# Layer 0's mixing by banks: each bank's first tiles followed by mixes of other tiles, two of four row statistics on the scalar engine, accumulators in the transposes' PSUM banks

## The chip, the cores and the metric

The kernel runs on one core of a Trainium2 chip. The metric is the time on the device in microseconds (us) of one execution; of several executions the median is taken. A core has five engines with instruction queues of their own, each worked off in order: PE (matrix products; PEld is its weight load), DVE (vector), ACT (scalar functions and copies), POOL (general, here elementwise work), and SP, which here only issues DMA transfers. They meet through semaphores. [...]

## The reference, cut to what matters

Two layers, each with a mixing (attention) and a feed-forward part, all with residuals, on x of 4 x 512 x 1024. The change is in the first part of layer 0 alone:

```
x = x + mix(layernorm(x))                 # the change is here
def mix(h):                               # h: 4 x 512 x 1024
    q = transpose(h, (2, 0, 1))           # 1024 columns, each 4 x 512
    prob = softmax(einsum('lnc,lmc->lnm', q, q) / sqrt(512))   # 4 x 4 for each column
    return h + transpose(einsum('lnm,lmc->lnc', prob, q), (1, 2, 0))
x = x + ffn0(layernorm(x))                # starts with normalise, transpose, matmul
```

For each of the 1024 columns the four batch rows are scored against one another over the 512 positions, and mixed by the softmax of the 4 x 4 scores.

## The kernel before, in words

x stays in SBUF as 16 tiles of 128 rows x 1024 columns: batch n (4) by position tile j (4), tile index 4n + j. For each j the four batches' rows are normalised into h (`normed_tiles`), with columns of the four batches side by side, in 32 groups of 128 (32 columns x 4 batches).

*Grams and turned h.* For each j, PE adds h·h of each group into `grams` (`gram`, L328), four PSUM banks g0 to g3 of 8 groups, and transposes each group (`turn`, L319) by four per PSUM bank (`pt`, 4 banks); ACT copies each bank into hTA (groups 0 to 19) or hTB (20 to 31) (L322). At the last j all grams are summed first, and then the eight turns follow.

*Weights.* `weights(gram)` makes the softmax of a bank on DVE: masked and reduced scores (L218, L222), maximum and difference (L224, L226), Exp on ACT (L227), sum, reciprocal, product with the reciprocal (pr, L233), plus the identity (L234), spread over halves (L236). `turned(halves, k)` expands half a bank into wt (L244), 128 x 512, for k = 0 on DVE and for k = 1 on POOL, lets PE transpose it (L252) and ACT copy it to w (L254). There are eight such w, q = 0 to 7; each has four groups.

*Mixing.* `mix(q, w, j)` is four products of hT with w into a PSUM tile of one bank (`ps`, L263) and an addition of it into x on DVE (L266). There are 8 x 4 = 32 of them. `ps` has 4 buffers that turned weights and mixes take in rotation: a buffer is free again once ACT has copied it or DVE has added it. The order: for each bank the weights, then for its two q the turn and the mix of tile j = 0 of the q before (L363 to L373); then the tiles j = 1 to 3 of q = 0 to 4 (the ones that read hTA), with the row statistics for the next layernorm of tiles n, j = 0 between them on DVE (`statistic`, L134: two bn_stats of 512 columns and their aggregate); then nine mixes of q = 5 to 7, which read hTB (L392).

*What lies beside it.* The feed-forward weights w0 come in 8 chunks of 128 x 1160 (`load_split`, L176): DMA to a staging tile, a cast to w_h on ACT (L182), the remainder w_l on POOL (L185). Chunks 0 to 3 use two staging buffers, so a transfer waits for POOL to have split the chunk two before. Chunks 4 to 7 and the first two normalised tiles (L141, L391) lie in the memory of hTA, so they wait for the last mix that reads hTA; they have three staging buffers. All four POOL wt come ahead of the splits in POOL's queue. The first feed-forward matmuls (L150 to L152, `matmul3`) need the transposes of a normalised tile (L163), a cast of these on ACT (L145) and the remainder hTl on DVE (L146); they take chunks 0 to 3 for all columns and then chunks 4 to 7.

*What sets the order.* The program is written through a scheduler that places instructions in each engine's queue by its own estimate; `tc.issue_after(i)` holds an instruction's place behind i in that order, and is no wait on the chip. `tops`, `wts`, `exps`, `rooted` are lists of instructions that such places refer to.

Of the kernel before, what the change touches and what calls it, by code (L numbers as in the profile page):

```python
# [17 lines left out]
P = 128  # L18
# [28 lines left out]
def block_kernel(ctx: ExitStack, tc: tile.TileContext, a: dict, out: bass.AP):  # L47
# [47 lines left out]
    def rsqrt(v, n, eps, name="y2", bufs=3):  # L95
# [10 lines left out]
        return y2  # L106

    def statistics(xs, tag="", bufs=3, junk=(), behind=None, gates=()):


        n = len(xs)
        mv = small.tile([P, n, 2], F32, name=f"mv{tag}", bufs=bufs)
        for k, xt in enumerate(xs):
            if k < len(junk):
                nm = small.tile([P, 1], F32, name="nm")
                with tc.issue_after(gates[0].ins) if gates else ExitStack():
                    A.activation(junk[k], xt, AF.Identity, scale=-1.0 / D, accum_out=nm)
                sq = small.tile([P, 1], F32, name="sq")
                A.activation(junk[k], xt, AF.Square, bias=nm, accum_out=sq)
                V.tensor_scalar(mv[:, k, 0:1], nm, -1.0, None, ALU.mult)  # L120
                V.tensor_scalar(mv[:, k, 1:2], sq, 1.0 / D, None, ALU.mult)
                continue
            st = small.tile([P, 2, 6], F32, name="st")
            for c in range(2):
                with tc.issue_after(gates[1].ins) if gates else ExitStack():
                    V.bn_stats(st[:, c, :], xt[:, c * 512 : (c + 1) * 512])
            summed = V.bn_aggr(mv[:, k, :], st)
        with ExitStack() if tag else tc.high_priority():
            if behind is not None:
                with tc.issue_after(summed.ins):  # L130
                    behind()
            return mv, rsqrt(mv[:, :, 1], n, 1e-5, f"rstd{tag}", bufs)
# [67 lines left out]
    with tc.tile_pool(name="a_hTB", bufs=1) as hTBp, tc.tile_pool(name="a_WB", bufs=GB // 4) as WBp, \  # L200
# [6 lines left out]
        def hT(g):  # L207
            return hTA[:, g, :] if g < GA else hTB[:, g - GA, :]

        exps = []  # L210
        tops, wts = [], []

        def weights(gram):
# [12 lines left out]
            tops.append(V.tensor_tensor(ex, sc, top.to_broadcast([P, GBK, NB]), ALU.subtract))  # L226
            exps.append(A.activation(ex, ex, AF.Exp, scale=1.0 / math.sqrt(S)))  # L227
            den = small.tile([P, GBK, 1], F32, name="den")
# [11 lines left out]

        def turned(halves, k, psp, Wp, eng):

            wt = wk.tile([P, 8 * NB, GL], F32, name="wt", bufs=3)
            made = eng.tensor_tensor(  # L244
                wt, halves[:, 4 * k : 4 * k + 4].rearrange("p g b m -> p (g b m)").unsqueeze(2)
                .to_broadcast([P, 8 * NB, GL]),
                same_col.unsqueeze(1).to_broadcast([P, 8 * NB, GL]), ALU.mult)
            wts.append(made)
            wt = wt.rearrange("p (g k) l -> p g (k l)", g=4)
            ps = psp.tile([P, 4, P], F32, name="ps")  # L250
            for g in range(4):
                T.transpose(ps[:, g, :], wt[:, g, :], ident)  # L252
            w = Wp.tile([P, 4, P], F32, name="w")
            A.copy(w, ps)  # L254
            return w, made

        xv = x.rearrange("p (n j) (k l) -> p j k n l", n=NB, l=GL)

        def mix(q, w, j, psp):

            ps = psp.tile([P, 4, P], F32, name="ps")
            for g in range(4):
                T.matmul(ps[:, g, :], lhsT=hT(4 * q + g)[:, j * P : (j + 1) * P], rhs=w[:, g, :],  # L263
                         start=True, stop=True)
            xs = xv[:, j, 8 * q : 8 * q + 8]
# [4 lines left out]
        with tc.tile_pool(name="a_h", bufs=2) as hp, tc.tile_pool(name="a_junk", bufs=1) as junkp:  # L270
# [3 lines left out]
            with tc.tile_pool(name="a_pt", bufs=4, space=PSUM, side="right") as ptp:  # L274
# [39 lines left out]
                for j in range(TPB):  # L314
# [17 lines left out]
                    if j == TPB - 1:  # L332


                        for q in range(NQ):
                            gram(q)
                        for q in range(NQ):
                            turn(q)
                        break
# [20 lines left out]

        with tc.tile_pool(name="a_ps", bufs=4, space=PSUM) as psp:
            ws = []
            for k, gram in enumerate(grams):  # L363
                halves = weights(gram)
                for i in range(2):
                    q = 2 * k + i
                    w, last_wt = turned(halves, i, psp, WAp if q < NQA else WBp, (V, G)[i])
                    ws.append(w)


                    if q > 0:
                        mix(q - 1, ws[q - 1], 0, psp)
            mix(NQ - 1, ws[NQ - 1], 0, psp)  # L373
            with tc.issue_after(exps[-1].ins):
                A.activation(first, first, AF.Sqrt)
            with tc.issue_after(last_wt.ins):
                load_w0(w0p, range(ND // 2), 2, (G, G))
            mv = small.tile([P, NB, 2], F32, name="mv", bufs=3)
            for k, (q, j) in enumerate((q, j) for q in range(NQA) for j in range(1, TPB)):
                mix(q, ws[q], j, psp)  # L380
                if k % 2 and k // 2 < NB:
                    statistic(mv, x[:, k // 2 * TPB, :], k // 2)
            stats0 = {0: (mv, rsqrt(mv[:, :, 1], NB, 1e-5, "rstd", 3))}
# [8 lines left out]
            for j in range(1, TPB):  # L392
                for q in range(NQA, NQ):
                    mix(q, ws[q], j, psp)
        psA.close()
        psB.close()
# [1333 lines left out]
```

## Time and profile before

| what | value |
|---|---|
| median of 3 runs | 1747.36 us (1746.56 to 1749.04) |
| the profiled execution, its own time | 1748.09 us |
| its span, first to last instruction | 1746.3 us |
| mean granted clock of PE over the span | 0.999 |
| end of layer 0's last transposes (L319) | 45.27 us |
| first turn of the weights (L252) | 46.32 us |
| first feed-forward transposes (L163) | 82.64 us |
| first feed-forward matmul (L150) | 85.19 us |

Times in the trace count from the first instruction. A line of a timeline is: start, length, engine, line of the program, operation, what it writes and reads, the shapes, how many were merged; in brackets, how long the engine was idle before it and what ended that. A PE record is one pass; an f32 product of 128 x 128 by 128 has two. A DVE length contains about 0.09 us that the next, independent operation overlaps: adds into x of 0.69 follow each other every 0.60. An operation of DVE or POOL that stands still after it was started is drawn as long, not as a gap. In the windows, the columns are: stretch, its length, busy time of PE, PEld, DVE, ACT, POOL with counts, PE's clock, the share of DMA and GB/s.

### The profile page before, as it was taken

The page shows a single profiled execution, that of the slowest core. Times are in us where ns is not written, and L with a number is a line of the kernel's source. Part 1 is how long each engine was busy: PE and PEld are TensorE (multiplying, and loading weights), DVE is VectorE, ACT ScalarE, POOL GpSimd, SP SyncE. Part 2 cuts the span into 40 slices and gives each one's busy share as a digit, 9 for nine tenths or more (in the row PEclk, how much of TensorE's full clock was granted, in tenths as well). Part 3 has the DMA queues.
Part 4 walks back from the last instruction along what each step waited for, and adds up shares of the span by engine and source line. Part 5 has one row for each costly group of instructions (what it writes and reads, how often), then busy time and mean ns, then how long its engine had stood idle before and what let it go on. Part 6 is the DMA issues. An engine that isn't in the chain of part 4 may idle for free.

```text
span 1746.3 us, 31628 instructions
## 1 busy us (share of the span) xinstructions
PE 1707.5 (98%) x10536; PEld 1429.7 (82%) x10536; DVE 1302.4 (75%) x3494; ACT 905.0 (52%) x2316; POOL 921.9 (53%) x926
## 2 busy tenths in 40 slices
PE   7999999999999999999999999999999999999999
PEld 6899999998677777767777767777767777789998
DVE  7977885676777777787777687777778776687675
ACT  7422331366765555575555575555476555453332
POOL 0553541203665665566566556566556655675454
PEclk9999999999999999999999999999999999999999
DMA  4313543245334234353333353342454333853431
GB/s 194 135 42 115 185 159 114 89 138 169 106 99 140 81 118 140 113 172 117 110 112 119 110 193 95 106 139 94 131 169 151 102 110 109 309 201 123 137 105 74
DMA packets 131939, 228.16 MB, mean 131 GB/s; under 512 B 22272, under 2 KB 58752, under 8 KB 128448
## 3 DMA queue, kind: packets, MB, share of 16 engines
q1 hardware_dynamic: 131776, 226.13, 39.2%
q8 instruction: 84, 1.38, 0.3%
q14 instruction: 79, 0.65, 0.1%
HBM read 156.60 MB, written 71.83 MB: 131 GB/s over the span
## 4 chain that ended last, share of the span: by engine, by line
PE 88%; DVE 5%; POOL 4%; ACT 2%; issue 1%; DMA 0%; POOLq 0%; ACTq 0%; DVEq 0%
PE psv L958 8%; PE pst L942 7%; PE po L150 4%; PE po L152 4%; PE po L151 4%; PE pss L150 4%; PE pss L151 3%; PE pss L152 3%; PE pob L150 3%; PE poa L150 3%; PE psq L150 3%; PE psq L152 3%; PE psq L151 3%; PE acc L150 3%; PE acc L152 3%; PE acc L151 3%
## 5 line engine op out<-in xcount | busy, mean ns | idle before, releaser
L921 ACT ACTIVATE p<-p,mn 128x512 f32<-128x512 f32 (+3 forms) x512 | 284.9, 559 | 211.4 <-DVE mn L918 210.8
L732 POOL TENSOR_TENSOR qf<-qf,ropeT 64x512 f32<-64x512 f32 x128 | 164.4, 1285 | 259.1 <-ACT qf L728 249.3
L918 DVE CUSTOM_DVE_ANT_0 p<-pss,causal 128x512 f32<-128x512 f32 (+3 forms) x512 | 232.7, 485 | 19.8 <-PE pss L152 15.8
L942 PE MATMUL pst<-ident,p 128*128 128x128 f32 x1280 | 185.9, 273 | 1.8 <-ACT pT L944 1.7
L733 POOL TENSOR_TENSOR qf<-qf,t 64x512 f32<-64x512 f32 x128 | 164.3, 1284 | 32.0 <-DVE t L731 23.8
L942 PEld LDWEIGHTS pst<-ident,p 128*128 128x128 f32 x1280 | 153.0, 141 | 29.6 <-ACT pT L944 4.8
L944 ACT COPY pT<-pst 128x512 f32<-128x512 f32 x256 | 142.1, 579 | 31.4 <-PE pst L942 29.5
L741 POOL TENSOR_TENSOR ql<-qf,qh 128x384 fp32r<-128x384 f32 x128 | 129.6, 1013 | 53.0 <-DVE qh L740 53.0
L150 PE MATMUL pss<-kT,ql 128*128 128x512 f32 (+2 forms) x384 | 143.6, 374 | 4.4 <-POOL ql L741 4.2
L993 POOL TENSOR_TENSOR cxl<-s,cxh 128x256 fp32r<-128x256 f32 x128 | 98.1, 773 | 85.2 <-ACT cxh L992 53.9
L150 PE MATMUL po<-w_h,hTl 128*128 128x384 f32 (+1 forms) x384 | 133.1, 347 | 0.7 <-DVE x L433 0.6
L151 PE MATMUL pss<-kT,qh 128*128 128x512 f32 (+2 forms) x384 | 130.4, 340 | 0.0
L152 PE MATMUL po<-w_h,hTh 128*128 128x384 f32 (+1 forms) x384 | 130.1, 339 | 0.0
L152 PE MATMUL pss<-kT,qh 128*128 128x512 f32 (+2 forms) x384 | 129.9, 338 | 0.0
L151 PE MATMUL po<-w_l,hTh 128*128 128x384 f32 (+1 forms) x384 | 129.7, 338 | 0.0
L944 DVE COPY pT<-pst 128x256 f32<-128x256 f32 x128 | 54.1, 423 | 97.8 <-PE pst L942 97.2
L728 ACT COPY qf<-psq 128x512 f32<-128x512 f32 x126 | 73.9, 587 | 69.7 <-PE psq L152 68.0
L730 DVE TENSOR_TENSOR t<-psq,ropeT 32x512 f32<-32x512 f32 x126 | 87.7, 696 | 24.5 <-ACT qf L728 20.2
L921 ACT ACTIVATION_READ_ACCUMULATOR p<-p,mn 128x1 f32 x512 | 97.2, 190 | 0.0
L150 PEld LDWEIGHTS pss<-kT,ql 128*128 128x128 f32 x384 | 72.1, 188 | 29.1 <-POOL ql L741 9.2
L731 DVE TENSOR_TENSOR t<-psq,ropeT 32x512 f32<-32x512 f32 x126 | 87.1, 691 | 1.7
L1035 DVE TENSOR_TENSOR xs<-xs,pob 128x512 f32<-128x512 f32 x105 | 71.1, 677 | 19.0 <-PE pob L152 18.8
(567 smaller groups left out, 4975.0 us busy)
## 6 DMA issues: line engine op xcount, KB each, us to landing
xs<-x_d SPq DMA_DIRECT2D x128, 256.0 KB
x_d<-xs SPq DMA_DIRECT2D x128, 256.0 KB
slotC<-in_woT_dram SPq DMA_DIRECT2D x32, 512.0 KB
rb<-r_d SPq DMA_DIRECT2D x128, 128.0 KB
w_t<-raw SPq DMA_DIRECT2D x32, 288.0 KB
x<-in_x_dram SPq DMA_DIRECT2D x16, 512.0 KB
x_d<-x SPq DMA_DIRECT2D x32, 256.0 KB
slotA<-q_d SPq DMA_DIRECT2D x8, 1024.0 KB
```

The costliest lines, as they stand in the source:

```text
L150: T.matmul(ps, lhsT=al, rhs=bh, start=start, stop=False, **kw)
L151: T.matmul(ps, lhsT=ah, rhs=bl, start=False, stop=False, **kw)
L152: T.matmul(ps, lhsT=ah, rhs=bh, start=False, stop=stop, **kw)
L732: G.tensor_tensor(f[mid], f[mid], ropeT[mid, 0, :], ALU.mult)
L733: G.tensor_tensor(f[mid], f[mid], t2[mid], ALU.add)
L741: G.tensor_tensor(l, f[:, P:S], f32(h), ALU.subtract)
L918: turn_of[0] = V.tensor_tensor_reduce(out=to, in0=ps[:, 0:n], in1=causal[:, S - n : S], scale=1.0, scalar=-NEG, op0=ALU.add, op1=ALU.min, ...
L921: A.activation(to, to, AF.Exp, bias=mn[:, i : i + 1], scale=-1.0, accum_out=rs[:, i : i + 1])
L942: T.transpose(ps[:, w : w + P], p[:, OF[i] + j * P : OF[i] + (j + 1) * P], ident)
L944: copy(pT[:, AT[js[0]] : AT[js[0]] + w], ps[:, 0:w])
L958: T.matmul(ps[n * KVR : (n + 1) * KVR, S - w : S], lhsT=k[:, j, :], rhs=pTs[u + n][:, AT[j] : AT[j] + w], start=(j == 0), stop=(j == TPB - 1))
L993: G.tensor_tensor(l, src, f32(h), ALU.subtract)
```

## The change

- `turned` is split: `expand` makes wt, `turned` transposes and copies it. The weights of the first two banks and the expansions of the first are written ahead of the last j's turns, so ACT's Exp of the second bank comes amid the copies of these.
- The loop over the banks: both turns of a bank, the two mixes of tile j = 0, then (except for the last bank) the next bank's weights and expansions and four mixes of other tiles of q = 0 to 3. The expansions of the last bank are both on DVE; POOL makes three wt instead of four.
- The first four chunks of w0 are loaded in two halves, at the first and the third bank. In POOL's queue the order becomes: two wt, the splits of chunks 0 and 1, the third wt, the splits of chunks 2 to 7. In ACT's queue the casts of chunks 0 and 1 come behind the first bank's two w copies and the third bank's Exp; the casts of chunks 2 and 3 come behind the second bank's w copies, the fourth bank's Exp and the table load, and ahead of the third bank's w copies.
- The statistics of n = 1 and 3 go to ACT (`act_statistic`: a pass for the mean, a pass for the squares, both into a PSUM tile that is not read), those of n = 0 and 2 stay on DVE. Three mixes of q = 4 stand between them. On DVE the two normalises for the feed-forward part come behind the additions of five of the nine last mixes, with four additions behind them (before: ahead of all nine).
- `ps` is allocated from the right side of PSUM, so that its four buffers take the transposes' banks in the transposes' order (before: from the left, in the opposite order).
- The number of products, of additions and of transfers is the same. Behind the first feed-forward matmul the order of every engine's instructions is the one before.

```diff
@@ -208,7 +211,7 @@
             return hTA[:, g, :] if g < GA else hTB[:, g - GA, :]
 
         exps = []
-        tops, wts = [], []
+        tops, wts, mixed, copied = [], [], [], []
 
         def weights(gram):
 
@@ -224,7 +227,8 @@
             V.tensor_reduce(top, sc, AX.X, ALU.max)
             ex = wk.tile([P, GBK, NB], F32, name="ex")
             tops.append(V.tensor_tensor(ex, sc, top.to_broadcast([P, GBK, NB]), ALU.subtract))
-            exps.append(A.activation(ex, ex, AF.Exp, scale=1.0 / math.sqrt(S)))
+            with tc.issue_after(copied[2 * len(exps) - 3].ins) if copied else ExitStack():
+                exps.append(A.activation(ex, ex, AF.Exp, scale=1.0 / math.sqrt(S)))
             den = small.tile([P, GBK, 1], F32, name="den")
             V.tensor_reduce(den, ex, AX.X, ALU.add)
             rden = small.tile([P, GBK, 1], F32, name="rden")
@@ -238,21 +242,24 @@
                             ALU.mult)
             return halves
 
-        def turned(halves, k, psp, Wp, eng):
+        def expand(halves, k, eng):
 
             wt = wk.tile([P, 8 * NB, GL], F32, name="wt", bufs=3)
-            made = eng.tensor_tensor(
+            wts.append(eng.tensor_tensor(
                 wt, halves[:, 4 * k : 4 * k + 4].rearrange("p g b m -> p (g b m)").unsqueeze(2)
                 .to_broadcast([P, 8 * NB, GL]),
-                same_col.unsqueeze(1).to_broadcast([P, 8 * NB, GL]), ALU.mult)
-            wts.append(made)
-            wt = wt.rearrange("p (g k) l -> p g (k l)", g=4)
+                same_col.unsqueeze(1).to_broadcast([P, 8 * NB, GL]), ALU.mult))
+            return wt.rearrange("p (g k) l -> p g (k l)", g=4)
+
+        def turned(wt, psp, Wp):
+
             ps = psp.tile([P, 4, P], F32, name="ps")
             for g in range(4):
-                T.transpose(ps[:, g, :], wt[:, g, :], ident)
+                with tc.issue_after(mixed[0].ins) if mixed else ExitStack():
+                    T.transpose(ps[:, g, :], wt[:, g, :], ident)
             w = Wp.tile([P, 4, P], F32, name="w")
-            A.copy(w, ps)
-            return w, made
+            copied.append(A.copy(w, ps))
+            return w
 
         xv = x.rearrange("p (n j) (k l) -> p j k n l", n=NB, l=GL)
 
@@ -260,8 +267,9 @@
 
             ps = psp.tile([P, 4, P], F32, name="ps")
             for g in range(4):
-                T.matmul(ps[:, g, :], lhsT=hT(4 * q + g)[:, j * P : (j + 1) * P], rhs=w[:, g, :],
-                         start=True, stop=True)
+                last = T.matmul(ps[:, g, :], lhsT=hT(4 * q + g)[:, j * P : (j + 1) * P],
+                                rhs=w[:, g, :], start=True, stop=True)
+            mixed[:] = [last]
             xs = xv[:, j, 8 * q : 8 * q + 8]
             V.tensor_tensor(xs, xs, ps.rearrange("p g c -> p (g c)")
                             .rearrange("p (k n l) -> p k n l", n=NB, l=GL), ALU.add)
@@ -334,8 +342,11 @@
 
                         for q in range(NQ):
                             gram(q)
+                        halves = weights(grams[0])
+                        pairs = [[expand(halves, i, (V, G)[i]) for i in range(2)]]
+                        halves = weights(grams[1])
                         for q in range(NQ):
-                            turn(q)
+                            turn(q, exps[1] if q >= NQ // 2 else None)
                         break
                     for q in range(NQ // 2):
                         turn(q)
@@ -358,28 +369,40 @@
                     w0.append(load_split(pool, stage, a["w0"][ch], [P, W0_COLS[-1][1]], f"w0{ch}",
                                          engines[ch % 2]))
 
-        with tc.tile_pool(name="a_ps", bufs=4, space=PSUM) as psp:
+
+        with tc.tile_pool(name="a_ps", bufs=4, space=PSUM, side="right") as psp:
             ws = []
-            for k, gram in enumerate(grams):
-                halves = weights(gram)
+            others = [(q, j) for q in range(4) for j in range(1, TPB)]
+            for k in range(len(grams)):
                 for i in range(2):
-                    q = 2 * k + i
-                    w, last_wt = turned(halves, i, psp, WAp if q < NQA else WBp, (V, G)[i])
-                    ws.append(w)
-
-
-                    if q > 0:
-                        mix(q - 1, ws[q - 1], 0, psp)
-            mix(NQ - 1, ws[NQ - 1], 0, psp)
+                    ws.append(turned(pairs[k][i], psp, WAp if 2 * k + i < NQA else WBp))
+                for q in (2 * k, 2 * k + 1):
+                    mix(q, ws[q], 0, psp)
+                if k + 1 == len(grams):
+                    break
+
+                if k > 0:
+                    halves = weights(grams[k + 1])
+                pairs.append([expand(halves, i, (V, G)[i and k < 2]) for i in range(2)])
+                if k in (0, 2):
+                    with tc.issue_after(wts[2 * k + 1].ins):
+                        load_w0(w0p, range(k, k + 2), 2, (G, G))
+                for q, j in others[4 * k : 4 * k + 4]:
+                    mix(q, ws[q], j, psp)
+            psA.close()
             with tc.issue_after(exps[-1].ins):
                 A.activation(first, first, AF.Sqrt)
-            with tc.issue_after(last_wt.ins):
-                load_w0(w0p, range(ND // 2), 2, (G, G))
+
             mv = small.tile([P, NB, 2], F32, name="mv", bufs=3)
-            for k, (q, j) in enumerate((q, j) for q in range(NQA) for j in range(1, TPB)):
-                mix(q, ws[q], j, psp)
-                if k % 2 and k // 2 < NB:
-                    statistic(mv, x[:, k // 2 * TPB, :], k // 2)
+            room = psB.enter_context(tc.tile_pool(name="a_jk", bufs=1, space=PSUM))
+            aj = room.tile([P, D], F32, name="aj")
+            for n in range(NB):
+                if n % 2:
+                    act_statistic(mv, x[:, n * TPB, :], n, aj)
+                else:
+                    statistic(mv, x[:, n * TPB, :], n)
+                if n:
+                    mix(4, ws[4], n, psp)
             stats0 = {0: (mv, rsqrt(mv[:, :, 1], NB, 1e-5, "rstd", 3))}
             aside.close()
             hp = wpools.enter_context(tc.tile_pool(name="b_h", bufs=2, side="right"))
@@ -392,7 +415,6 @@
             for j in range(1, TPB):
                 for q in range(NQA, NQ):
                     mix(q, ws[q], j, psp)
-        psA.close()
         psB.close()
 
 
```

More of the change, by code (lines that the diff above doesn't have):

```diff
@@ L106, in rsqrt, with act_statistic @@
         return y2
+    def act_statistic(mv, xt, k, junk, gates=()):
+        nm = small.tile([P, 1], F32, name="nm")
+        with tc.issue_after(gates[0].ins) if gates else ExitStack():
+            A.activation(junk, xt, AF.Identity, scale=-1.0 / D, accum_out=nm)
+        sq = small.tile([P, 1], F32, name="sq")
+        A.activation(junk, xt, AF.Square, bias=nm, accum_out=sq)
+        V.tensor_scalar(mv[:, k, 0:1], nm, -1.0, None, ALU.mult)
+        V.tensor_scalar(mv[:, k, 1:2], sq, 1.0 / D, None, ALU.mult)
     def statistics(xs, tag="", bufs=3, junk=(), behind=None, gates=()):
@@ L114, in statistics @@
             if k < len(junk):
[L115 to L121, printed above, removed]
+                act_statistic(mv, xt, k, junk[k], gates[:1])
                 continue
```

## Prediction

> **What bounds the kernel now.** I read the page's shares first. TensorE (PE) is busy 98% of the span and 88% of the chain that ended last is its own work, so a microsecond counts only if PE stands still for it or runs at a lower clock.
>
> ```profile
> PE 1707.5 (98%) x10536; PEld 1429.7 (82%) x10536; DVE 1302.4 (75%) x3494; ACT 905.0 (52%) x2316; POOL 921.9 (53%) x926
> ...
> PE 88%; DVE 5%; POOL 4%; ACT 2%; issue 1%; DMA 0%; POOLq 0%; ACTq 0%; DVEq 0%
> ```
>
> The change lies between the end of layer 0's transposes (45.27 us in the trace) and the first feed-forward matmul (85.19); behind that each engine's order of instructions is the old one. Next I read the windows there (PE, PEld, DVE, ACT, POOL busy, then PE's clock) and PE's timeline.
>
> ```profile
> 49.00:57.00 8.00, 6.42 (x43) 6.42 (x44) 7.04 (x15) 4.82 (x8) 4.40 (x4) 0.79 0.10 42
> 57.00:74.00 17.00, 17.00 (x154) 17.00 (x154) 16.16 (x32) 4.28 (x6) 10.19 (x4) 1.00 0.23 72
> ```
>
> ```profile
> 46.32 1.09 PE L252 MATMUL ps<-ident,wt 128*128 128x128 f32 x8 [1.05 <-ACT hTB L322]
> 47.71 1.16 PE L263 MATMUL ps<-w,hTA 128*128 128x128 f32 x8 [0.29 <-ACT w L254]
> 50.58 1.04 PE L252 MATMUL ps<-ident,wt 128*128 128x128 f32 x4 [1.71 <-DVE wt L244]
> ...
> 61.20 13.56 PE L263 MATMUL ps<-w,hTA 128*128 128x128 f32 x120
> 74.60 8.20 PE L263 MATMUL ps<-w,hTB 128*128 128x128 f32 x72
> 82.64 1.04 PE L163 MATMUL pt<-ident,h 128*128 128x128 f32 x8
> 84.78 0.66 PE L163 MATMUL pt<-ident,h 128*128 128x128 f32 x4 [1.10 <-DVE hTl L146]
> ```
>
> From 57 on PE has no gap, and one mix (8 records) takes 0.893 us (120 records in 13.4). A turn (4 records) takes 0.437. Eight turns and 32 mixes are 3.5 + 28.6 = 32.1 us; the stretch 45.27 to 82.64 has 37.4. So 5.3 us can be won at most: 3.05 of gaps, and the clock of 0.79 behind the 1.71 us gap, 8 x 0.21 = 1.7 us.
>
> Last I read VectorE (DVE) against GpSimd (POOL). First POOL's timeline, then DVE's:
>
> ```profile
> 56.63 5.28 POOL L185 TENSOR_TENSOR w_l<-stage,w_h 128x1160 fp32r<-128x1160 f32 x2
> ...
> 80.10 10.59 POOL L185 TENSOR_TENSOR w_l<-stage,w_h 128x1160 fp32r<-128x1160 f32 x4 [8.77 <-ACT w_h L182]
> 90.64 1.27 POOL L484 TENSOR_TENSOR raw<-raw 128x288 fp32r<-128x288 f32 x1
> ```
>
> ```profile
> 75.65 1.54 DVE L141 TENSOR_SCALAR h<-x,mv,rstd 128x1024 f32<-128x1024 f32 x2
> ...
> 90.15 1.09 DVE L141 TENSOR_SCALAR h<-x,mv,rstd 128x1024 f32<-128x1024 f32 x1
> 91.16 0.20 DVE L138 BATCH_NORM_AGGREGATE mv<-st 128x2 f32<-128x12 f32 x1
> 91.28 1.17 DVE L141 TENSOR_SCALAR h<-x,mv,rstd 128x1024 f32<-128x1024 f32 x1
> ...
> 103.50 6.43 DVE L525 SCALAR_TENSOR_TENSOR eq<-lg,best,rank 128x8 f32<-128x8 f32 x1
> ```
>
> A normalise takes 0.8 us with POOL idle (75.65). At 90.15 it ends 0.55 behind POOL's w_l (90.69), and the next ends 0.54 behind POOL's raw (91.91): it stood still until POOL was through. POOL's raw took 1.27 there, and 0.81 at 106.32, so it waited in turn. DVE's products of two SBUF tensors behave alike: halves at 50.44 took 1.08 instead of 0.22, ending with POOL's wt of 49.87. The adds into x (one input in PSUM) and the bn_stats between 56.6 and 62 keep their 0.69 under w_l.
>
> **The change part by part.**
>
> *Banks in order.* The first turn no longer waits for the eighth copy, only for the fifth: it starts at 45.1. The first mix still needs eight ACT copies at 0.48, an Exp and its own w copy, so about 46.9 instead of 47.71: −0.8.
>
> *Six mixes behind a pair of turns* (two of the first tile, four others). By 52.2 PE has work where it had the 1.71 gap and the slow clock: −3.4. The smaller waits behind ACT's w (0.29) stay, about 0.5 at the last pair, which has nothing behind it. Gross gain 4.2.
>
> *ACT's queue.* The casts of w0 chunks 2 and 3 now stand ahead of the third pair's w copies. Chunk 2's transfer may start when POOL has split chunk 0, chunk 3's when it has split chunk 1. Before, chunk 2 went out at 59.33 and its cast began at 64.82 (5.5 later), chunk 3 at 61.94 and 66.21 (4.3). Chunk 0's cast can begin at about 49.2 (its data were there by 49.1), its split at 50.4, so the splits end at 53.1 and 55.8 at the earliest, chunk 3 lands at 60.1 and its cast ends at 61.2. The w copies then end at 61.7. Unhindered, PE would have turned this pair by 59.4 and mixed at 59.9: +1.8, even without any lock. That leaves a net gain near 2 at most.
>
> *POOL's queue.* Two w_l of 2.65 us now stand ahead of the third pair's wt, from about 50.4 to 56, and two more follow near 60 to 65. Before, all weights were done on DVE (54.28) when w_l began (56.63), so no row has just this meeting. Its price from both sides: nothing, if all of DVE's two-input products (wt, pr, pr+same_n, halves, for the last two banks) fall between; a w_l each otherwise. Behind a blocked product stand the adds into x, and for those PE, whose four PSUM buffers are full after four mixes.
>
> [...] The row at 103.50 differs: it held through nine POOL instructions in a row. But the DVE operations of 95.31 to 100.17 got in at the next end each time. I take the rule: the third bank's wt blocked to 53.0, then an add each 0.6, a PE gap of 1.6 before the second pair's second turn; a PE gap of 1.2 near 66 by the last wt; some of ACT's 1.8 hides behind these (1.5 left). Losses 4.3 + 0.2 of small waits against the gain of 4.2: the mixes end at +0.3, I take +0.5. If halves is caught by the first w_l and wt by the second, the gap is 4.4 and slows the clock: +3.7. By the nine-instruction row it would be +8. If nothing meets, −1.7.
>
> *Statistics on ACT.* Four bn_stats (0.6 each) leave DVE; ACT takes four passes of about 1.2. They can't start before the first tile's eighth mix is added. That was at 62.1, twenty microseconds ahead of the mixes' end; now twelve mixes follow it, 10.7 us. Let H be the end of the last mix that reads hTA (74.6 before, nine mixes from the end in both). The eighth add ends at H−1.7, ACT's passes at H+3.5, root and the four small DVE operations between the adds put the first normalise at H+5.9. w_l of chunk 4 starts at H+5.5, as before (80.10), since its transfer waits for H alone. Before, the normalises ran at 75.65, with POOL idle; now the first finds w_l running. It goes at H+8.1 for 0.55, POOL's second w_l takes its turn (2.65), the second normalise ends at H+11.8. Four adds of 0.6 stand behind it, then hTl (0.67) and a turn: the first feed-forward matmul at H+15.3, where it was 85.19 − 74.6 = 10.6. That is +4.7. If the two normalises go through together it is +2.4; if the first beats w_l and both run, +0.3.
>
> *Clock.* With PE idle for some 5 us from H+9.7, the next stretch at half clock is likely, as after 48.87 (1.7 us lost there). Part of it is idle anyway: +1.0, between 0 and 1.7.
>
> Sum: 0.5 + 4.7 + 1.0 = +6.2. The profiled execution took 1748.09 us, its span 1746.3; 1748.1 + 6.2 = 1754.3 on that footing. It lies 0.7 above the median of 1747.36, so the median I forecast is 1753.6. Everything behind this stretch keeps its order, and PE's gaps up to 330 us sum to under 2 us, so little is absorbed.
>
> **The rivals.**
>
> 1. *The forecast*, 1753.6: chance 0.45.
> 2. *The normalises slip through together*, tail +2.4, clock +0.5, mixes +0.5: 1750.8. For it: DVE has both at the head of its queue. Against: POOL's raw got in between two of them at 91. Chance 0.15.
> 3. *The mixes are held twice* (halves by one w_l, wt by the next): 3.7 + 4.7 + 1.7 = +10, 1757.5. The order of halves and w_l at 50.4 is a matter of 0.2 us. Chance 0.18.
> 4. *The other side: DVE and POOL don't meet*, because DVE's products fall between w_l, and the first normalise starts before the w_l of chunk 4, which it must beat by more than the 0.4 I find missing. Then −1.7 in the mixes and +0.3: 1746.0, and if the casts land early enough to leave ACT free as well, −3.5 to −4: 1743.5. Chance 0.22, of which 0.1 for the latter.
>
> **How the numbers follow.** This kernel's measurement tells 0.2% (3.5 us) from no change. Faster by that needs rival 4 with ACT free: 0.10. Within: the rest of 4 and most of 2: 0.24. Slower: 0.66. The range reaches from rival 4 without ACT's gain, 1745.5, to a little over rival 3, 1758.5.
>
> **What would show it.** Right: a DVE wt or halves of 2 us or more while w_l runs between 50 and 56; ACT's w copy of the third pair waiting behind two casts; both early normalises 1 to 3 us long against w_l after 80; a PE gap of 3 us or more before the third group of feed-forward transposes, with a clock under 1 behind it. Wrong: DVE's products keeping 0.2 and 0.7 us under w_l, or the normalises starting before chunk 4's split; then the mixes end near 80 and the time falls.

## The result, and the profile after

| | before | after |
|---|---|---|
| median of 6 runs, us | 1748.2 (1746.56 to 1749.04) | 1758.7 (1756.94 to 1761.8) |
| ratio, 95% interval | | 1.0061 [1.0048, 1.0074] |
| the profiled execution, its span | 1748.09, 1746.3 | 1756.94, 1755.2 |
| first turn of the weights | 46.32 | 46.41 |
| end of the mixes that read hTA | 74.60 | 77.98 |
| first feed-forward matmul | 85.19 | 93.42 |

The change makes the kernel slower: 10.5 us by the medians, 8.9 by the two profiled executions. The forecast was +6.2; the time lies 0.2 us above the range. Matched PE instruction by PE instruction, the distance of the two traces is 3.4 us at the end of the hTA mixes, 8.2 at the first feed-forward matmul, 8.9 at 115 us, and 8.4 to 9.1 from there to the end. All of it arises in the stretch that the change rearranges. (The profiled execution was the fastest of the six after. Why the medians lie 1.6 further apart isn't shown by any trace here.)

First the page after: the shares of busy time, then the chain that ended last. PE works 3 us more (at a lower clock), and its part of the chain is smaller.

```profile
PE 1710.4 (97%) x10536; PEld 1432.7 (82%) x10536; DVE 1305.1 (74%) x3493; ACT 909.6 (52%) x2324; POOL 921.5 (53%) x925
...
PE 83%; DVE 5%; POOL 4%; ACT 1%; DMA 1%; issue 1%; SPq 0%; POOLq 0%; ACTq 0%; DVEq 0%
```

The windows after, with PE's clock as third last column. Between 57 and 74 the clock was 1.00 before and is 0.83; behind 86 it is 0.76.

```profile
49.00:57.00 8.00, 5.36 (x46) 4.96 (x45) 7.93 (x11) 2.84 (x3) 6.71 (x3) 0.93 0.17 55
57.00:74.00 17.00, 16.57 (x121) 16.03 (x120) 13.50 (x23) 6.46 (x10) 5.27 (x2) 0.83 0.16 62
...
86.00:100.00 14.00, 8.59 (x44) 8.10 (x43) 13.64 (x21) 5.30 (x9) 10.27 (x7) 0.76 0.43 143
```

PE's timeline after:

```profile
46.41 1.09 PE L259 MATMUL ps<-ident,wt 128*128 128x128 f32 x8 [1.16 <-ACT hTB L330]
47.79 5.62 PE L270 MATMUL ps<-w,hTA 128*128 128x128 f32 x48 [0.29 <-ACT w L261]
53.55 0.66 PE L259 MATMUL ps<-ident,wt 128*128 128x128 f32 x4
56.71 1.09 PE L259 MATMUL ps<-ident,wt 128*128 128x128 f32 x4 [2.50 <-DVE x L274]
57.59 7.97 PE L270 MATMUL ps<-w,hTA 128*128 128x128 f32 x48
...
77.98 8.20 PE L270 MATMUL ps<-w,hTB 128*128 128x128 f32 x72
...
92.65 1.12 PE L166 MATMUL pt<-ident,h 128*128 128x128 f32 x4 [4.93 <-DVE hTl L149]
93.42 0.68 PE L153 MATMUL po<-w_h,hTl 128*128 128x392 f32 x1
```

Six mixes (48 records) do run behind the first pair without a gap. Then the second pair's second half stands still for 2.50 us, and the next six mixes take 7.97 us for the work of 5.62. The same again at the tail: 4.93 us of idle time, and then a matmul of 0.68 where it was 0.42.

Who holds PE there is read from POOL's and DVE's timelines side by side.

```profile
50.17 5.25 POOL L188 TENSOR_TENSOR w_l<-stage,w_h 128x1160 fp32r<-128x1160 f32 x2 [1.32 <-ACT w_h L185]
...
83.33 11.39 POOL L188 TENSOR_TENSOR w_l<-stage,w_h 128x1160 fp32r<-128x1160 f32 x4 [16.88 <-ACT w_h L185]
```

```profile
50.64 2.27 DVE L240 TENSOR_TENSOR halves<-pr,same_half 128x64 f32<-128x64 f32 x1
...
53.42 2.54 DVE L248 TENSOR_TENSOR wt<-halves,same_col 128x512 f32<-128x512 f32 x1
55.89 1.27 DVE L274 TENSOR_TENSOR x<-x,ps 128x512 f32<-128x512 f32 x2
...
83.59 6.02 DVE L144 TENSOR_SCALAR h<-x,mv,rstd 128x1024 f32<-128x1024 f32 x2
89.53 2.47 DVE L274 TENSOR_TENSOR x<-x,ps 128x512 f32<-128x512 f32 x4
91.92 1.28 DVE L149 TENSOR_TENSOR hTl<-pt,hTh 128x512 fp32r<-128x512 f32 x2
```

Both products are the third bank's. halves (0.22 us when POOL is idle, by the run e1 below) ends at 52.90, when the first w_l ends (52.82); wt (0.7) ends at 55.97, where the second ends (55.42) plus most of its own length. The adds that PE waits for stand in between. At 83.59 the two normalises, 0.8 us each with POOL idle, take 2.98 and 3.12; four adds, and only then hTl, come behind them.

**The theory to test** (theory 1): both losses are one thing, DVE operations that stand still while a w_l of 2.65 us runs on POOL (below, such an operation is *held*, and the encounter of the two is a *meeting*), and what PE loses behind that, the stretches at half clock included. Rivals: the order of the mixes, ACT's casts ahead of the w copies, statistics on ACT that come late.

### The profile page after: what moved, and what is told of

Same layout as the page of the kernel before. It is cut to its first block, busy times and chain, and to the rows that moved or that the text cites. A ratio compares the mean times of both kernels' runs of the same rounds, so it can differ in the third digit from the quotient of the medians.

```text
span 1755.2 us, 31632 instructions
## 1 busy us (share of the span) xinstructions
PE 1710.4 (97%) x10536; PEld 1432.7 (82%) x10536; DVE 1305.1 (74%) x3493; ACT 909.6 (52%) x2324; POOL 921.5 (53%) x925
## 4 chain that ended last, share of the span: by engine, by line
PE 83%; DVE 5%; POOL 4%; ACT 1%; DMA 1%; issue 1%; SPq 0%; POOLq 0%; ACTq 0%; DVEq 0%
PE psv L980 8%; PE pst L964 7%; PE po L153 4%; PE po L155 4%; PE po L154 4%; PE pss L153 4%; PE pss L154 3%; PE pss L155 3%; PE pob L153 3%; PE poa L153 3%; PE psq L153 3%; PE psq L155 3%; PE psq L154 3%; PE pob L155 3%; PE pob L154 3%; PE poa L155 3%
```

## The experiments

All runs in one table. H is the end of the mixes that read hTA, F the first feed-forward matmul, both in us of the trace; the last column is for how long PE's clock was at half between 45 and 100 us, by the clock's record in the trace. The ratio is to the kernel before, whose median lay between 1748.0 and 1748.5 beside all of them. In e3 the first turn came at 47.80, at least a microsecond later than in all other runs, so its H and F lie that much too late.

| run | median | ratio [95%] | H | F | F−H | half clock |
|---|---|---|---|---|---|---|
| before | 1748.2 | | 74.60 | 85.19 | 10.6 | 3.41 |
| after | 1758.7 | 1.0061 [1.0048, 1.0074] | 77.98 | 93.42 | 15.4 | 13.65 |
| e1 late loads | 1755.8 | 1.0044 [1.0031, 1.0057] | 76.52 | 92.03 | 15.5 | 10.24 |
| e2 normalises on ACT | 1758.5 | 1.0059 [1.0045, 1.0072] | 76.72 | 93.13 | 16.4 | 13.65 |
| e3 both | 1757.0 | 1.0048 [1.0035, 1.0061] | 76.08 | 92.50 | 16.4 | 10.24 |
| e4 w_l in four | 1752.9 | 1.0028 [1.0016, 1.0039] | 78.19 | 89.62 | 11.4 | 10.24 |
| e5 statistics on DVE | 1759.5 | 1.0064 [1.0051, 1.0077] | 77.78 | 95.80 | 18.0 | 10.24 |
| e6 one PSUM pool | 1758.3 | 1.0056 [1.0044, 1.0069] | 77.78 | 90.71 | 12.9 | 6.83 |
| e7 e4, casts last | 1749.0 | 1.0004 [0.9995, 1.0013] | 72.70 | 85.10 | 12.4 | 3.41 |
| e8 e7, two mixes, one pool | 1747.3 | 0.9994 [0.9986, 1.0003] | 73.10 | 83.61 | 10.5 | 0 |
| e9 casts last alone | 1759.0 | 1.0058 [1.0046, 1.0071] | 77.23 | 95.09 | 17.9 | 13.65 |
| e10 before, w_l in four | 1747.9 | 1.0000 [0.9991, 1.0009] | 74.77 | 85.36 | 10.6 | 0 |
| e11 e8 with three mixes | 1746.6 | 0.9990 [0.9981, 0.9999] | 73.28 | 83.78 | 10.5 | 0 |
| e12 e11, w_l whole | 1751.1 | 1.0015 [1.0006, 1.0024] | 77.14 | 87.65 | 10.5 | 3.41 |

### Take the meeting out of the mixes (e1)

```diff
-                if k in (0, 2):
-                    with tc.issue_after(wts[2 * k + 1].ins):
-                        load_w0(w0p, range(k, k + 2), 2, (G, G))
...
+            seen = wk.tile([P, GL], F32, name="seen", bufs=1)
+            with tc.issue_after(wts[5].ins):
+                gate = G.tensor_tensor(seen, last_wt[0][:, 0, 0:GL], same_col, ALU.mult)
+            with tc.issue_after(gate.ins):
+                load_w0(w0p, range(ND // 2), 2, (G, G))
```

> The changed kernel with w0's chunks 0 to 3 all loaded, cast and split behind the last of the layer's weights: POOL makes its three wt, then waits for DVE's last wt, and only then splits. Theory 1 (meeting): the mixes lost their gain because w_l on POOL stood against DVE's halves and wt (2.27 and 2.54 us). Then halves is back near 0.2 to 1.1 us and wt near 0.7 to 1.5, the 2.50 us gap before the second half of the second bank's turns goes with the half clock behind it (2.6 us), and the hTA mixes end near 73 instead of 77.98. The early normalises still meet w_l (chunks 0 to 3 are split later now), so the tail keeps its excess of about 4.7; time 1752 to 1755. Rival (order): PE waits because six mixes and the four PSUM buffers need the adds in this order, whatever POOL does: the 2.5 us gap stays, the mixes end at 77 to 78, 1757 to 1760. Rival (casts): the time was lost to ACT's casts in front of w copies; that goes here too, so this run alone does not separate it from theory 1, the length of halves and wt does.

The splits now begin at 62.17, when all weights are made. halves took 0.22 and wt 0.68 us, by DVE's timeline:

```profile
50.90 0.22 DVE L240 TENSOR_TENSOR halves<-pr,same_half 128x64 f32<-128x64 f32 x1
...
51.63 0.68 DVE L248 TENSOR_TENSOR wt<-halves,same_col 128x512 f32<-128x512 f32 x1
```

PE's gap of 2.50 and the half clock behind it are gone, and three pairs of turns with their mixes, and the fourth pair's turns, run from 46.5 to 67.9 with no gap over 0.3. So the order of the mixes isn't what holds PE. H is still 76.52 and not 73, and the time 0.8 us above what was expected, because a new wait came up at the last pair. PE's timeline, then ACT's:

```profile
70.32 2.83 PE L272 MATMUL ps<-w,hTB 128*128 128x128 f32 x16 [2.43 <-ACT w L263]
```

```profile
68.62 1.16 ACT L185 CAST w_h<-stage 128x1160 fp32r<-128x1160 f32 x1 [6.79 <-DMA stage<-in_w_dram]
69.69 1.07 ACT L263 COPY w<-ps 128x512 f32<-128x512 f32 x2
```

The w copies stand behind a cast of chunk 2, which waited 6.79 us for its transfer. In the program that transfer waits for POOL to have split chunk 0; the two w_l from 62.17 took 5.25, so that was near 64.8. It is the forecast's cast term, in another place. The tail is as long as before the edit.

### Take the normalises off DVE (e2, and e3 with e1's edit)

```diff
+            off2 = small.tile([P, 3], F32, name="off")[:, 0:2]
+            V.scalar_tensor_tensor(out=off2, in0=stats0[0][0][:, 0:2, 0], scalar=-1.0,
+                                   in1=stats0[0][1][:, 0:2], op0=ALU.mult, op1=ALU.mult)
...
-                done = normalise(early[n], x[:, n * TPB, :], *stats0[0], n)
+                done = A.activation(early[n], x[:, n * TPB, :], AF.Identity, bias=off2[:, n : n + 1],
+                                    scale=stats0[0][1][:, n : n + 1])
```

> The changed kernel with the two early normalises as ACT activations (Identity with a scale and a bias), everything else kept. Theory 1: the mixes stay at 78 (their meeting is untouched), but no normalise is held (2.98 and 3.12 us before), the four adds run behind the mixes at once, and the first feed-forward matmul comes 11 to 12.5 us behind the end of the hTA mixes instead of 15.4; with the second half-clock window gone or smaller 3.5 to 5 us are won: 1753 to 1755. Rival (late statistics): the tail is long because two tiles' statistics on ACT come late, not because the normalises are held: then ACT's normalises start where DVE's did and the next operations win at most 1 us: 1757 to 1759.

> Both edits of the two runs before together. Theory 1: the mixes end near 73, 1.7 us earlier than before the change, and the feed-forward's first matmul comes 11 to 12.5 us later, at 84 to 86 (85.19 before the change): the whole loss of about 10 us goes, 1746 to 1749, and the two gains add up. Rival: if something other than the meetings of POOL and DVE causes a part (the order of the mixes, ACT's queue), 3 us or more of the loss stay: 1750 to 1754.

Both expectations failed: the tail got no shorter (16.4). DVE's timeline of e2 shows why, and ACT's what it did to the normalise:

```profile
82.53 2.29 DVE L105 SCALAR_TENSOR_TENSOR rstd<-nt,y 128x4 f32<-128x4 f32 x1
...
85.34 2.06 DVE L413 SCALAR_TENSOR_TENSOR off<-mv,rstd 128x2 f32<-128x2 f32 x1
```

```profile
87.44 1.24 ACT L417 ACTIVATE h<-x,off,rstd 128x1024 f32<-128x1024 f32 x1 [4.01 <-DVE off L413]
```

The hold moved to the next DVE operations with two inputs in SBUF. rstd, 4 elements a row and 0.16 us elsewhere, stood for 2.29 behind one w_l, and off for 2.06 behind the other. So here an operation of four elements a row was held for over 2 us. The normalise on ACT then began 3.9 us later than DVE's had. This is a failure of the edit, not of theory 1, but it left the cause of the tail unproved.

### Shorten the POOL instruction instead (e4)

```diff
                     w0.append(load_split(pool, stage, a["w0"][ch], [P, W0_COLS[-1][1]], f"w0{ch}",
-                                         engines[ch % 2]))
+                                         engines[ch % 2], 4))
```

> The changed kernel with each w_l of w0 in four instructions of 290 columns in place of one of 1160: the same POOL work, the same places. If a held DVE instruction goes when the running POOL instruction ends, no hold is longer than about 0.7 us: halves and wt fall from 2.3 and 2.5 to under 1.3 us, the normalises from 3.0 to under 1.8, and most of the loss goes, 1748 to 1752. If DVE stays held while POOL has more in its queue (as one DVE instruction did for 6.43 us at 103.50 before the change), the holds stay at 2 us and more and the time at 1757 to 1760. If four instructions cost POOL much more than one (over 3.2 us together instead of 2.65), splits later in the kernel come late as well and the time can be worse.

DVE's timeline, in the mixes and at the tail:

```profile
50.57 0.78 DVE L240 TENSOR_TENSOR halves<-pr,same_half 128x64 f32<-128x64 f32 x1
...
51.87 0.71 DVE L248 TENSOR_TENSOR wt<-halves,same_col 128x512 f32<-128x512 f32 x1
...
83.79 2.37 DVE L144 TENSOR_SCALAR h<-x,mv,rstd 128x1024 f32<-128x1024 f32 x2
```

Same POOL work in the same places, in quarters of 0.8 us: halves fell from 2.27 to 0.78, wt from 2.54 to 0.71, the normalises from 6.0 together to 2.4, F−H from 15.4 to 11.4. Both holds are thereby shown, and that a hold ends when the running POOL instruction ends, and not when its queue is empty: here eight quarters stood in it, over 6.60 us. (The one row before the change that stood through nine POOL instructions, 6.43 us at 103.50, isn't explained by this; no operation in this stretch did so in any run.) The time, 1752.9, is 0.9 above what was expected. POOL was delayed in turn: the sixteen quarters from 83.60, with the normalises among them, took 13.19 us, where the eight from 62.15 took 6.16; so about 0.9 us of waiting, an estimate from these two.

The 2.50 us gap went as expected, but H did not move. PE's timeline at the third pair, then ACT's:

```profile
63.98 2.08 PE L270 MATMUL ps<-w,hTA 128*128 128x128 f32 x8 [3.15 <-ACT w L261]
```

```profile
60.92 1.16 ACT L185 CAST w_h<-stage 128x1160 fp32r<-128x1160 f32 x1 [4.51 <-DMA stage<-in_w_dram]
62.28 1.16 ACT L185 CAST w_h<-stage 128x1160 fp32r<-128x1160 f32 x1 [0.20 <-DMA stage<-in_w_dram]
63.34 1.06 ACT L261 COPY w<-ps 128x512 f32<-128x512 f32 x2
```

Its turns were done at 60.8, on time; the w copies stood on ACT behind the casts of chunks 2 and 3 (60.92 to 63.44), which waited for their transfers.

### ACT's casts, with and without the hold (e7, e9)

Both place the casts of chunks 2 and 3 behind the last w copies; e7 has w_l in four, e9 has it whole. The new last argument of `load_w0` is what the casts' place in ACT's queue is held behind.

```diff
-                if k in (0, 2):
-                    with tc.issue_after(wts[2 * k + 1].ins):
-                        load_w0(w0p, range(k, k + 2), 2, (G, G))
+                if k == 0:
+                    with tc.issue_after(wts[1].ins):
+                        load_w0(w0p, range(2), 2, (G, G))
...
+            load_w0(w0p, range(2, 4), 2, (G, G), copied[-1])
```

> The run with w_l in four parts, and in addition ACT's casts of w0's chunks 2 and 3 placed behind the last of the weights' copies (only the casts wait; the transfers stay early). In the run with four parts the first mix of the third pair waited 3.15 us for its w, which stood behind the two casts, and 2 us more went at half clock. Theory 1 with the cast term of the forecast: that gap goes, PE runs from 47.6 to the end of the mixes with no gap over 0.4, the hTA mixes end near 72.3 instead of 78.2, 5 to 6 us are won and the time is 1746 to 1748.5. Rival: the third pair is late for another reason (its weights on DVE, the adds), and the gap stays at 2 us or more: 1751 to 1753.

> The changed kernel with w_l whole (one instruction of 1160 columns) and only ACT's casts of w0's chunks 2 and 3 placed behind the last of the weights' copies. Theory 1: in the changed kernel the casts cost nothing, because the third pair is already late by the hold of halves and wt; the 2.50 us gap before the second bank's second half stays, the hTA mixes end between 77 and 78.5 and the tail keeps its length, 1756 to 1760. Rival: the casts cost in the changed kernel already, what they cost without the hold (the 3.15 us gap of the run with four parts); then 3 to 5 us are won here, 1753 to 1756.

e7: PE ran from 46.54 to the end of the mixes with no gap over 0.3, and H is 72.70, 5.5 us earlier than in e4; the time is 0.5 above what was expected. Of the 10.5 us, 1.0 is left, which the interval doesn't tell from nothing. e9: the gap of 2.50 stayed, and the time didn't change. DVE's timeline of e9, then ACT's of the changed kernel:

```profile
53.71 2.54 DVE L249 TENSOR_TENSOR wt<-halves,same_col 128x512 f32<-128x512 f32 x1
...
82.58 2.54 DVE L105 SCALAR_TENSOR_TENSOR rstd<-nt,y 128x4 f32<-128x4 f32 x1
```

```profile
59.97 2.20 ACT L185 CAST w_h<-stage 128x1160 fp32r<-128x1160 f32 x2
66.04 1.07 ACT L261 COPY w<-ps 128x512 f32<-128x512 f32 x2 [3.87 <-PE ps L259]
```

e9 alone isn't a clean comparison: H came 0.75 earlier, with 3.41 us at half clock behind the gap instead of 6.83, and the tail got 2.5 longer, as rstd was held too. But the changed kernel's own lines say the same: its casts ended at 62.17, and ACT then stood idle for 3.87 until PE's turns gave it something to copy. So in the changed kernel the casts cost nothing, because the hold came first; without the hold they cost 5.5 us of H (e4 against e7). One loss hid the other.

### The parts that cost nothing (e5, e6)

e5 puts all four statistics on DVE; e6 lets turns and mixes take their accumulators from the transposes' own pool.

```diff
-                if n % 2:
-                    act_statistic(mv, x[:, n * TPB, :], n, aj)
-                else:
-                    statistic(mv, x[:, n * TPB, :], n)
+                statistic(mv, x[:, n * TPB, :], n)
```

```diff
-        with tc.tile_pool(name="a_ps", bufs=4, space=PSUM, side="right") as psp:
+        with psC:
+            psp = ptp
```

> The changed kernel with all four statistics of layer 0's first feed-forward step on DVE, as they were before the change; the rest kept. It asks whether moving two tiles' statistics to ACT is what makes the tail long. Theory 1: no; the normalises start about 0.7 us earlier or later than 83.6 and still meet the w_l of chunk 4, so the time stays within 3 us of the changed kernel's 1758.7: 1755 to 1761. Rival (late statistics on ACT): DVE's own statistics are ready before chunk 4's w_l, the normalises take 0.8 us each, the first feed-forward matmul comes 11 us behind the end of the hTA mixes and 4 to 5 us are won, 1753 to 1755.

> The changed kernel with the turns and mixes allocating their accumulators from the transposes' own pool, so that they follow it buffer by buffer. The forecast gave the bank order 0.8 us by an earlier first turn; in the profile after, that turn still waits for the eighth of the layer's copies. If a new pool waits for the whole old one, the first turn comes near 45.1 here and the first mix near 46.9 (0.8 us earlier), and the time falls by 1 us at most: 1757 to 1759. If the wait has another cause, the first turn stays at 46.4 and nothing changes. Whether the later meetings of DVE and POOL shift with it is open; they decide more than the 0.8.

e5: the time stayed; rstd was held for 2.14 us and the normalises for 5.65, from 86.33. The statistics on ACT aren't the cause; they even spare DVE work that here made the last mixes wait (0.52 and 0.60 us for adds).

e6: PE's and DVE's timelines:

```profile
45.17 1.06 PE L259 MATMUL pt<-ident,wt 128*128 128x128 f32 x8
46.98 5.62 PE L270 MATMUL pt<-w,hTA 128*128 128x128 f32 x48 [0.75 <-ACT w L261]
```

```profile
51.07 2.29 DVE L237 TENSOR_TENSOR pr<-ex,rden 128x32 f32<-128x32 f32 x1
53.39 2.55 DVE L238 TENSOR_TENSOR pr<-pr,same_n 128x32 f32<-128x32 f32 x1
```

The first turn comes at 45.17 and the first mix at 46.98, as the forecast had it for the change itself. With the change's own new pool on the other side of PSUM the first turn waited for the eighth copy, as before. But PE's 0.8 us were lost again at once: two other products, pr twice, were now caught in place of halves and wt, and the same w_l cost a gap of 3.64 us. Being earlier by a fraction of a us didn't evade a queue of 5.24 us. At the tail the first normalise slipped ahead of w_l by 0.15 us and took 0.81, the second was held for 3.15: F−H 12.9.

### A control, and versions without either meeting (e10, e8, e11, e12)

e10 is the kernel before with e4's edit. e8 and e11 are e7 with e6's pool and fewer mixes of other tiles behind each pair (two, three), the rest behind the last pair; e12 is e11 with w_l whole. The diff of e11 against e7, without the pool:

```diff
-                for q, j in others[4 * k : 4 * k + 4]:
+                for q, j in others[3 * k : 3 * k + 3]:
...
+            rest = others[9:] + [(4, j) for j in range(1, TPB)]
+            step = len(rest) // 3
...
-                    mix(4, ws[4], n, psp)
+                    for q, j in rest[(n - 1) * step : n * step]:
+                        mix(q, ws[q], j, psp)
```

> The kernel before the change with each w_l of w0 in four instructions of 290 columns, nothing else. A control: if four parts won time by themselves, the runs with four parts would owe it to that and not to shorter holds. Before the change no DVE product that PE waited for met a w_l, so by theory 1 nothing changes: 1746.5 to 1749.5. If the time falls by 2 us or more, part of the gain of the runs in four parts is of another kind.

> The run before it in this list, with two mixes of other tiles behind each pair instead of four, the rest of them behind the last pair around the statistics, and the accumulators from the transposes' pool. The first tile's last mix then comes 6 mixes (5.4 us) earlier before the end of the mixes, so the statistics and the two normalises are done while PE still mixes. Theory 1: if the weights keep pace (PE gaps under 1 us in all), the mixes end near 72, the first feed-forward matmul comes at most 10.6 us later as before the change, and the time is 1743 to 1746. Rival: with only four mixes behind a pair the weights are late for each bank (gaps of 1 us and more, with half clock behind them), and the time is 1747 to 1752.

> As the run with two mixes behind each pair (four parts, casts last, the transposes' pool), with three mixes behind each pair. In the run with two, PE still waited 0.49 and 0.77 us for the second and third pair's w and ran with no half clock; the normalises were done at 75.4, three us ahead of chunk 4's w_l at 78.6. With three behind, these gaps should shrink to about 0.25, and the normalises come 2.7 us later, still ahead of w_l by a few tenths: the first feed-forward matmul near 82.8 instead of 83.6, 1745.5 to 1747.5. Rival: the normalises slip behind the first w_l, are held 1.2 us each and the adds behind them come late, as in the run with four mixes behind: a tail longer by 1 to 2 us, a half-clock stretch behind it, 1748 to 1750.

> The run with three mixes behind each pair, with w_l whole again (one instruction of 1160 columns). It separates the two meetings: here the normalises come ahead of chunk 4's w_l, so only the meeting between the splits of chunks 0 and 1 and the second bank's DVE products is left. Theory 1: one or two of these products (pr, halves or wt) are held about 2.3 us each, PE stops for 2 us or more before the second bank's turns, and the hTA mixes end 2.5 to 5 us later than the 73.28 of the run in four parts; the tail stays 10.5 us; 1748.5 to 1752. Rival: once the normalises are early and the casts last, nothing that PE waits for meets w_l any more, and four parts are not needed: 1745.5 to 1747.5.

e10: no difference (ratio 1.0000). Four parts won nothing where nothing that PE waits for is held, so e4's gain is that of the shorter holds.

e8 and e11: the first tile's last mix comes earlier before H, so both normalises are done before chunk 4's first w_l (78.74 in e11). DVE's timeline of e11:

```profile
76.20 1.53 DVE L144 TENSOR_SCALAR h<-x,mv,rstd 128x1024 f32<-128x1024 f32 x2
```

F−H is 10.5 again, and F 83.8. e11 is the only run that is faster than the kernel before, by 1.5 us, with an interval that ends just below 1. Two expectations were missed: e8's time lies 1.3 us above what was expected, and in e11 the second and third pair still waited 0.84 and 0.75 us instead of 0.25. e12 gives the price of the mixes' meeting alone. DVE's timeline:

```profile
51.16 2.12 DVE L238 TENSOR_TENSOR pr<-ex,rden 128x32 f32<-128x32 f32 x1
53.31 2.55 DVE L239 TENSOR_TENSOR pr<-pr,same_n 128x32 f32<-128x32 f32 x1
```

pr (the third bank's; the expectation calls it the second's) was held twice, PE stood still for 3.93 us, H came 3.9 us later than in e11 and the time 4.5.

## Why the prediction was wrong

The direction was right, and so was the mechanism of both losses (DVE held by w_l, in the mixes and at the tail); the step that failed is the size of the mixes' term. In the order of its steps, in us of the two profiled executions:

- *Banks in order, −0.8*: failed. The first turn waited for the eighth copy (46.41 against 46.32). e6 shows that the gain exists, 47.79 to 46.98 for the first mix, but it takes one pool for both uses.
- *Six mixes behind a pair, −3.4*: too much. With w_l in four and the casts last (e7: halves 0.72, wt 0.71) H falls from 74.60 to 72.70, with the first turn 0.2 later: about −2. PE still waits for a w copy in each of the four banks, 1.0 in all.
- *ACT's casts, +1.8*: the right mechanism, and more than that once it shows (3.15 and the half clock behind it, e4), but nothing in the changed kernel (its own ACT lines, and e9); the forecast's sign, the third pair's w copies waiting behind two casts, did not come. That the term hides behind the holds was said of 0.3 of it; all of it did.
- *The mixes' end, +0.5*: this is the step that failed; it was +3.4. The forecast had w_l begin near 50.4, let halves pass, let wt be caught once, and added 1.2 for the last wt. On the chip w_l began at 50.17 and halves at 50.64; halves was caught by the first w_l and wt by the second, as in the forecast's third rival (+3.7, chance 0.18), while the last bank's wt passed freely (its halves was held for 2.07 at 61.85, which nobody waited for). The gap was 2.50 instead of that rival's 4.4, and the rest is clock: 7.97 − 5.62 = 2.35 us. 2.50 + 2.35 and 0.5 on the slow half turn make 5.3 of loss, against 1.9 of gain. The clock's part is of this execution: behind the same gap of 2.5 the six mixes took 6.48 in e2, 7.10 in e5 and 7.22 in e9.
- *What the forecast could have had for the mixes' end*: of the third bank's four products (pr twice, halves, wt) two were caught in all six runs whose two first w_l stood whole in that place, halves and wt in four of them, pr twice in e6 and e12, where they came later against the queue. No run shows the forecast's case, in which halves slips through and wt alone is caught, nor its gaps of 1.6 and 1.2 us: after the change PE's gap was 2.50, and the last bank's two wt took 0.77 and 0.68. That a hold ends with the running w_l, from which the forecast had its 53.0, no run had shown for this meeting then; after the change halves ended at 52.90, w_l at 52.82, and e4's quarters bear it out.
- *The tail, +4.7*: right in place, order and size. The forecast had the normalises from H + 5.9 to H + 11.8 and the first matmul at H + 15.3; they ran from H + 5.6 to H + 11.6, and it came at H + 15.4. That the size fits so well is in part luck: rstd, right before them, began within 0.01 us of w_l and passed in 0.15; in e5 and e9 it was held for 2.14 and 2.54 and the tail was 18.0 and 17.9 long, while in e6 one normalise slipped ahead and it was 12.9. The forecast had no term for rstd. That it is the w_l that costs is shown by e4 (11.4) and by e8, e11 and e12 (10.5), where the normalises come first.
- *Clock behind the tail, +1.0*: what is left, 8.9 − 3.4 − 4.85 = 0.65.

The sum of the profiled terms, 3.4 + 4.85 + 0.65, is 8.9 against 6.2; the mixes' term, 2.9 too small, is the difference (the other two together were 0.2 too large). The forecast then went from the profiled execution to the median by taking 0.7 off; the median after lies 1.8 above its own profiled execution. Without that, the time would have been inside the range. No run shows what makes it so; the cause of these 1.8 stays open.

## What to carry to other kernels

Ahead of moving elementwise work on GpSimd, list the VectorE instructions that the bounding engine waits for and that are of the kinds held here: operations with two inputs in SBUF, down to rstd's four elements (2.14 to 2.54 us instead of 0.16), and the normalise (2.98 and 3.12 instead of 0.8). Two other kinds ran on under w_l after the change: the adds into x, with one input in PSUM (0.68 at 52.82), and the bn_stats (0.69 at 63.85). Of a chain of four products, two queued w_l caught two in each of six runs; by these, reckon with one for each long GpSimd instruction queued. Cutting the GpSimd instruction into parts took 5.8 us off (e4) and cost no time where nothing was held (e10), though GpSimd itself worked longer (6.13 us for two w_l in e11, 5.27 in e12); placing the dependent work before the queue, as with the normalises of e11, is as good. When an edit removes a loss and the time stays, look for the loss that stood behind it before giving up the theory, as with e4's casts.

## What the runs showed beyond that

*Half clock came in multiples of 3.41 us.* By the clock's record PE's clock in this stretch was at half once for 3.41 us before the change, and twice for 6.83 after it. In the runs it was 0, 3.41, 6.83 or 10.24 us in the mixes and again at the tail: in e2, for one, the mean clocks of 0.97, 0.92 and 0.63 in the windows 45 to 57, 57 to 74 and 86 to 100 make 3.4 and 10.4. A gap of 1.71 us brought 3.41 before the change and none in e10, where the same gap came 0.5 us later; 2.35 brought none in e3; 2.50 brought 6.83 after the change and 3.41 in e9, as did 2.49 in e2 and e5; 3.93 brought 3.41 in e12. Gaps up to 1.02 (e8, e11) brought none. So behind the gaps near 2 us the clock cost anything from nothing to about the gap's own length again (1.7 behind 1.71 before the change, 2.35 behind 2.50 after it), and a forecast should carry both. What decides between them isn't shown.

*A new PSUM pool did not follow the old one buffer by buffer here*: 1.2 us for the first turn (46.41 after the change, 45.17 in e6).
